# The head of a load queue: image 0's first 32 rows in three transfers of 8, 8 and 16 rows instead of one

## The chip, the cores and the metric

One core of a Trainium2 chip runs the program. The time is device microseconds of one execution; medians of several runs are given. The profile's span is about 1.2 us shorter than that time (82.0 us against 83.26 in the run that was profiled before the change), and all instants below are counted from the span's start.

The engines' names: PE is TensorE, DVE VectorE, ACT ScalarE, POOL GpSimd; SP (SyncE) only issues transfers. A transfer is cut into packets, which the 16 DMA engines of the core move. It has landed when all 16 have added to its semaphore. The records name neither the engine of a packet nor that of a landing; where this text speaks of one engine's lag, it goes by the order of the 16 landings.

## The reference, cut to what matters

```
x: (8, 32, 128, 128) float32
out = x + conv3x3(groupnorm(x, 16 groups), weight, bias)      # padding 1
```

The convolution is written with an FFT of 256 and a crop that begins at 64, so that only a part of the image gets anything from it. The kernel holds each image as 128 partitions (channel, row parity, column parity) of 64 x 64 numbers. Each image's statistics are needed before its convolution, and all 16.8 MB are read and written once.

## The kernel before

SP issues all loads at the start, in order: image 0 in two halves of 32 rows (1 MB each, 8,192 bytes per partition), images 1 to 3 (2 MB each), two pairs (4 MB each). Each load has a semaphore of its own. ACT issues the weights. (Here and below `[...]` marks a cut.)

```python
    def load(to, of, by="sp"):
        name = f"load{len(put.sems)}"
        put.semaphore(name)
        return put(by, lambda e: e.dma_start(to, of), adds=name)

    loaded[0] = []
    for half in range(2):
        rows = slice(half * H // 2, (half + 1) * H // 2)
        loaded[0].append((rows.stop, load(xts[0][:, rows, :], x[0, :, 0, rows, :])))
        if half == 0:
            weights_in = load(wb_sb, wb, by="act")
    for img in range(1, 4):
        loaded[img] = [(H, load(xts[img], x[img // 2, :, img % 2]))]
    for pair in range(2, NPAIR):
        loaded[2 * pair] = loaded[2 * pair + 1] = [(H, load(pairs[pair], x[pair]))]
```

The first consumers are sums (DVE) and sums of squares (ACT) of image 0's first half, then of its second half, then the normalization and the convolution on TensorE. Before the convolution TensorE does a small matmul on image 1's first element, so it waits for image 1 as well. Results are written in place and stored by SP:

```python
    def pilot(img):
        pilot_ok[img] = put(
            "pe", lambda e: e.matmul(ps_w[:, img : img + 1], avg, xts[img][:, 0, 0:1], start=True, stop=True),
            *rows_in(img, 1), avg_ok, mark=True,
        )
    # [...]
    group(0, 1)
    warm_ok = keep_warm(0, 1, w_ok)
    pilot(1)
    take_std(0)
    normalize(0)
    # [...] per image: multiply, add, store
            if img == 2 or img == 4:
                store(out[img // 2 - 1], pairs[img // 2 - 1], *finished(img - 2, img - 1))
```

## Time and profile before

| | before |
|---|---|
| time, median of 3 runs | 83.2 us (83.17 to 83.45) |
| span | 82.0 us |
| bytes moved | 33.62 MB, 410 GB/s over the span |
| DMA engines busy | 97.2% of the span on average |
| first packet; last landing | 1.84 us; 81.96 us |

The prediction shows the lines and how to read them. The point to hold on to: the 16 DMA engines are busy without a pause from 2.5 to 80.5 us, so the time is the length of the transfer stream.

### The profile page before, as it was taken

How to read it: one execution, taken by the hardware profiler on the slowest of the kernel's cores; microseconds unless marked ns; L12 is line 12 of the kernel's file. 1: busy time of each engine (PE TensorE's matmuls, PEld its weight loads, DVE VectorE, ACT ScalarE, POOL GpSimd, SP SyncE). 2: the span in 40 equal slices, each digit the busy share in tenths (PEclk: the TensorE clock that was granted, in tenths of full speed). 3: DMA queues.
4: the chain of work that ended last, by engine and by line, in shares of the span. 5: the costliest groups of instructions: out<-in, count | busy, mean ns of one | idle time of the engine just before them, and what ended most of it. 6: DMA issues, size and time to landing. Idle time of an engine off the chain costs nothing.

```text
span 82.0 us, 686 instructions
## 1 busy us (share of the span) xinstructions
PE 66.8 (81%) x222; PEld 41.3 (50%) x222; DVE 50.2 (61%) x43; ACT 47.9 (58%) x53; POOL 31.6 (39%) x43
## 2 busy tenths in 40 slices
PE   0009974999999999999999999999999999993000
PEld 0005433566666666666666656666666666660000
DVE  0009936960899499769949995996899324006000
ACT  3307967981699299569947974994798260000000
POOL 6876000004069900106992930490085029400000
PEclk9999998579999999999999999999999999999965
DMA  2899999999979979979959889989979999999995
GB/s 40 299 415 443 463 415 423 447 407 423 551 304 511 479 320 479 511 336 431 511 256 511 383 383 511 447 352 479 463 336 423 423 431 439 431 423 419 397 430 239
DMA packets 2164, 33.62 MB, mean 410 GB/s; under 512 B 296, under 2 KB 330, under 8 KB 500
## 3 DMA queue, kind: packets, MB, share of 16 engines
q1 hardware_dynamic: 2020, 33.36, 96.3%
q0 software_dynamic: 96, 0.19, 0.6%
q10 hardware_dynamic: 48, 0.06, 0.3%
HBM read 16.84 MB, written 16.78 MB: 410 GB/s over the span
## 4 chain that ended last, share of the span: by engine, by line
PE 74%; DMA 14%; DVE 2%; SPq 1%; issue 0%
PE ps L412 73%; DMA x<-x_dram 14%; DVE x L428 2%; PE ps_m L318 1%; SPq L183 1%; PE ps_w L265 0%
## 5 line engine op out<-in xcount | busy, mean ns | idle before, releaser
L412 PE MATMUL ps<-g,w_sb 128*128 128x363 f32 (+1 forms) x192 | 60.7, 473 | 0.1
L412 PEld LDWEIGHTS ps<-g,w_sb 128*128 128x128 f32 x192 | 36.1, 194 | 20.0 <-ACT origin L292 1.4
L283 DVE TENSOR_REDUCE sums<-x 128x1 f32<-128x4096 f32 x7 | 30.9, 4411 | 0.6 <-DMA x<-x_dram 0.6
L394 POOL TENSOR_SCALAR x<-x,bias_sb 128x1984 f32<-128x1984 f32 (+3 forms) x12 | 23.2, 1945 | 18.9 <-ACT origin L292 14.6
L303 ACT ACTIVATE unused<-x,origin 128x4096 f32<-128x4096 f32 (+1 forms) x9 | 30.0, 3330 | 0.3
L428 DVE SCALAR_TENSOR_TENSOR x<-ps,bias_sb,x 128x1089 f32<-128x1089 f32 (+2 forms) x9 | 10.9, 1220 | 7.7 <-PE ps L412 7.7
L373 ACT ACTIVATE g<-x,rstd 128x1089 f32<-128x1089 f32 (+2 forms) x8 | 9.4, 1190 | 3.4 <-DVE rstd L347 3.4
L283 DVE TENSOR_REDUCE first_sums<-x 128x1 f32<-128x2048 f32 x2 | 4.6, 2286 | 6.2 <-DMA x<-x_dram 6.2
L258 POOL COPY sums<-x 128x1 f32<-128x1 f32 x6 | 1.0, 186 | 18.2 <-DMA x<-x_dram 18.2
L335 DVE TENSOR_SCALAR var<-ps_m,square 128x1 f32<-128x1 f32 x8 | 1.8, 219 | 8.2 <-ACT square L330 8.2
L265 PE MATMUL ps_w<-x,avg 128*128 128x1 f32 x4 | 0.9, 304 | 7.1 <-POOL w_sb L476 6.1
L330 ACT ACTIVATE square<-ps_m,origin 128x1 f32<-128x1 f32 x8 | 2.1, 261 | 7.3 <-PE ps_m L318 7.3
L447 PE MATMUL ps<-x,avg 128*128 128x512 f32 x6 | 4.9, 942 | 0.0
L265 PEld LDWEIGHTS ps_w<-x,avg 128*128 128x128 f32 x4 | 0.8, 248 | 7.9 <-POOL w_sb L476 6.1
L318 PEld LDWEIGHTS ps_m<-sums,avg 128*128 128x128 f32 x16 | 2.8, 188 | 2.2 <-DVE x L428 1.0
L341 ACT ACTIVATE std<-var,eps 128x1 f32<-128x1 f32 x8 | 2.4, 294 | 2.3 <-DVE var L335 2.3
L344 DVE RECIPROCAL rstd<-std 128x1 f32<-128x1 f32 x8 | 1.3, 164 | 2.9 <-ACT std L341 2.9
L292 ACT ACTIVATE origin<-ps_w 128x1 f32<-128x1 f32 x2 | 0.3, 160 | 4.0 <-PE ps_w L265 4.0
L476 POOL COPY w_sb<-wb_sb 32x128 f32<-32x128 f32 (+1 forms) x8 | 2.5, 340 | 0.0
L318 PE MATMUL ps_m<-sums,avg 128*128 128x3 f32 x16 | 2.3, 214 | 0.0
L447 PEld LDWEIGHTS ps<-x,avg 128*128 128x128 f32 x6 | 1.5, 287 | 1.0 <-issue 1.0
L237 ACT ACT_TABLE_LOAD x1 | 1.3, 1283 | 1.2 <-PEq L579 1.2
(21 smaller groups left out, 13.3 us busy)
## 6 DMA issues: line engine op xcount, KB each, us to landing
x<-x_dram SPq DMA_DIRECT2D x2, 4096.0 KB, 34.3
out_dram<-x SPq DMA_DIRECT2D x2, 4096.0 KB
x<-x_dram SPq DMA_DIRECT2D x3, 2048.0 KB, 16.0
out_dram<-x SPq DMA_DIRECT2D x3, 2048.0 KB
x<-x_dram SPq DMA_DIRECT2D x2, 1024.0 KB, 6.2
out_dram<-x SPq DMA_DIRECT2D x1, 1056.0 KB
out_dram<-x SPq DMA_DIRECT2D x1, 800.0 KB
out_dram<-x POOLq DMA_DIRECT2D x1, 189.0 KB, 7.7
```

The lines of the kernel that those rows point to most:

```text
L283: lambda e: e.tensor_reduce(to_sum(img, k)[:, 0:1], piece, mybir.AxisListType.X, ALU.add),
L303: lambda e: e.activation(unused[:, rows.start * W : rows.stop * W], piece, AF.Square, bias=origins[img], accum_out=to_sum(img, k)[:, 1:2],),
L318: lambda e: e.matmul(ps_ms[:, 0 : of.shape[1]], avg, of, start=(part == 0), stop=(part == last)),
L330: lambda e: e.activation(squares[img], ps_ms[:, 0:1], AF.Square, bias=origins[img]),
L335: lambda e: e.tensor_scalar(variances[img], ps_ms[:, 1:2], squares[img], None, op0=ALU.subtract),
L341: lambda e: e.activation(stds[img], variances[img], AF.Sqrt, bias=eps, scale=float(FFT * FFT)),
L373: lambda e: e.activation(g[:, rows, :], xt[:, LO + rows.start : LO + rows.stop, LO:W], AF.Identity, bias=rstd[:, 1:2], scale=rstd[:, 0:1],),
L394: put("pool", lambda e: e.tensor_scalar(part, part, 1.0, bias_sb, op0=ALU.mult, op1=ALU.add), *free, mark=mark)
L412: lambda e, k=k, dc=dc, rows=rows, top=top: e.matmul(ps[:, 0:rows, 0 : N - dc], w_sb[:, k * P : (k + 1) * P], g[:, top : top + rows, dc:N] ...
L428: lambda e: e.scalar_tensor_tensor(part, in0=ps, scalar=bias_sb, in1=part, op0=ALU.add, op1=ALU.add),
L447: "pe", lambda e: e.matmul(pss[1][:, 0, :], avg, piece, start=True, stop=True),
L476: lambda e: e.tensor_copy(w5[to, :, dc, :, c.start * C : c.stop * C], taps[:, 1 - rin : 5 - rin, b, :].rearrange("p (dr r) b o -> p dr r ( ...
```

## The change

The intent, as it can be read from it: begin with small transfers, so that the stream gets going sooner, and grow them. The consumers still wait for all three (the semaphore counts to 48). The weights' load is written first, which changes nothing in its queue.

```diff
+PIECES = (8, 8, 16), (32,)
 [...]
-    def load(to, of, by="sp"):
+    def load(*transfers, by="sp"):
         name = f"load{len(put.sems)}"
         put.semaphore(name)
-        return put(by, lambda e: e.dma_start(to, of), adds=name)
-
-    loaded[0] = []
-    for half in range(2):
-        rows = slice(half * H // 2, (half + 1) * H // 2)
-        loaded[0].append((rows.stop, load(xts[0][:, rows, :], x[0, :, 0, rows, :])))
-        if half == 0:
-            weights_in = load(wb_sb, wb, by="act")
+
+        return [put(by, lambda e: e.dma_start(to, of), adds=name) for to, of in transfers][-1]
+
+    weights_in = load((wb_sb, wb), by="act")
+
+    loaded[0], first = [], 0
+    for pieces in PIECES:
+        transfers = []
+        for piece in pieces:
+            rows = slice(first, first + piece)
+            transfers.append((xts[0][:, rows, :], x[0, :, 0, rows, :]))
+            first = rows.stop
+        loaded[0].append((first, load(*transfers)))
 [...]  # the other loads pass their pair of patterns as one argument
```

More of the change, by code (lines that the diff above doesn't have):

```diff
@@ L178, in conv_preact_kernel @@
     loaded = {}
-    def load(to, of, by="sp"):
+    def load(*transfers, by="sp"):
         name = f"load{len(put.sems)}"
         put.semaphore(name)
-        return put(by, lambda e: e.dma_start(to, of), adds=name)
-    loaded[0] = []
-    for half in range(2):
-        rows = slice(half * H // 2, (half + 1) * H // 2)
-        loaded[0].append((rows.stop, load(xts[0][:, rows, :], x[0, :, 0, rows, :])))
-        if half == 0:
-            weights_in = load(wb_sb, wb, by="act")
+        return [put(by, lambda e: e.dma_start(to, of), adds=name) for to, of in transfers][-1]
[8 more added lines that the diff above has]
+        loaded[0].append((first, load(*transfers)))
     for img in range(1, 4):
-        loaded[img] = [(H, load(xts[img], x[img // 2, :, img % 2]))]
+        loaded[img] = [(H, load((xts[img], x[img // 2, :, img % 2])))]
     for pair in range(2, NPAIR):
-        loaded[2 * pair] = loaded[2 * pair + 1] = [(H, load(pairs[pair], x[pair]))]
+        loaded[2 * pair] = loaded[2 * pair + 1] = [(H, load((pairs[pair], x[pair])))]
     def rows_in(img, last):
```

## The prediction

> **What bounds the kernel now.** I read the page's clock and DMA rows first, then the DMA queues, then stretches of time, and only then the chain of waits, because a kernel that moves 33.6 MB in 82 us is a suspect for being limited by the DMA engines however busy TensorE looks.
>
> The page, parts 1 to 3: TensorE's busy share, then (in slices of 2.05 us) the granted clock, the DMA engines' busy share and the rate, then the queues with their share of all 16 engines' time.
>
> ```profile
> PE 66.8 (81%) x222; PEld 41.3 (50%) x222; DVE 50.2 (61%) x43; ACT 47.9 (58%) x53; POOL 31.6 (39%) x43
> ...
> PEclk9999998579999999999999999999999999999965
> DMA  2899999999979979979959889989979999999995
> ...
> q1 hardware_dynamic: 2020, 33.36, 96.3%
> q0 software_dynamic: 96, 0.19, 0.6%
> q10 hardware_dynamic: 48, 0.06, 0.3%
> HBM read 16.84 MB, written 16.78 MB: 410 GB/s over the span
> ```
>
> The shares of the queues add up to 97.2% of the span: on average each DMA engine is busy for 79.7 of 82.0 us. Stretches of time (columns: stretch, length, busy us of PE, weight loads, DVE, ACT, POOL, granted clock, DMA share, GB/s) show where the other 2.3 us lie:
>
> ```profile
> 0.00:1.80 1.80, 0.00 (x0) 0.00 (x0) 0.00 (x0) 0.55 (x1) 1.11 (x7) 1.00 0.00 0
> 1.80:3.00 1.20, 0.00 (x0) 0.00 (x0) 0.00 (x0) 0.93 (x2) 1.05 (x3) 1.00 0.90 179
> 3.00:13.40 10.40, 5.76 (x13) 2.81 (x13) 5.21 (x6) 5.43 (x8) 3.93 (x15) 1.00 1.03 435
> 13.40:42.00 28.60, 28.53 (x97) 18.13 (x97) 22.95 (x16) 21.96 (x23) 11.26 (x9) 0.94 1.00 423
> 42.00:79.50 37.50, 32.55 (x116) 20.35 (x115) 22.06 (x22) 19.01 (x21) 14.23 (x12) 0.99 1.00 430
> 79.50:82.00 2.50, 0.00 (x0) 0.00 (x0) 0.00 (x0) 0.00 (x0) 0.00 (x0) 0.50 0.63 267
> ```
>
> The reader is to see three things: nothing moves before 1.8 us; from 1.8 to 3.0 the engines count as busy at 179 GB/s only (a slow start); from 3.0 to 79.5 their share is 1.00 or more (a packet is booked where it begins) at 423 to 435 GB/s. The single packet records say the same: the first begins at 1.84, in every whole microsecond from 2.5 to 80.5 the 16 engines are busy, the last ends at 81.62. So the transfer stream never runs dry, and the kernel is as long as that stream.
>
> The chain of waits tells another story, and I do not follow it:
>
> ```profile
> 1.73 11.62 DMA x<-x_dram
> 13.34 0.04 issue
> 13.39 0.38 PE ps_w L265 x2
> 13.77 0.07 issue
> 13.84 6.14 PE ps L412 x14
> ...
> 71.55 3.01 PE ps L412 x10
> 74.56 0.02 issue
> 74.58 1.48 DVE x L428 x2
> ```
>
> It passes from image 1's landing through TensorE without a gap to the last add at 76.06; the last store is issued after that, and all lands at 81.96. But the last store is 1,056 KB, which at 430 GB/s takes 2.5 us, not 5.9. It stands behind earlier stores: its first data packet begins at 77.98 in the packet records. A transfer's first packet came 1.02 us after its issue began (0.81 to 1.84), so a store issued at 76.09 could have begun at about 77.1. TensorE's chain thus has some 0.9 us to spare at the end, the tightest place; the other stores are issued 2.7 us or more before the transfers in front of them have landed.
>
> **What the Trainium skill says.** (1) "DMA: Bandwidth & Descriptors", section "Why a DMA increments its semaphore by 16 and not by 1": with two transfers in flight on one semaphore a count that would suit the first alone may be filled by the second; only the sum of all is safe. The change waits for the sum, 48, so it is correct, and nothing can start after the first 8 rows. The trace agrees on the counting: one load gives 16 landings (5.53 to 5.97 us for the first). (2) Same page, "Why small descriptors are slow (HBM only)": each packet has a fixed cost. The trace agrees and sizes it: packets of 32,768, 16,384, 8,192 and 1,984 bytes took 1,213, 611, 309 and 81 ns in steady flow, a line of 0.0367 ns per byte plus 8 to 9 ns. (3) Same page, "Latency and other measured facts": about 0.6 us to the first byte. Here the first packet came 0.64 us after the issuing instruction ended (1.20 to 1.84). (4) "TensorE: Matmul & The Clock Gate", Part 1: windows of 3.4 us that run freely. In this trace the first convolution's matmuls run at half clock from 13.83 to 17.24, a whole window; other executions may lose less, but by the paragraph above that time is hidden.
>
> **The change part by part.** The weights' load is written first in the program, but it was and is issued on ACT's queue at 0.81, beside SP's first: nothing moves. SP's order stays image 0, image 0, image 1 and so on. One 1 MB transfer of the first half (128 rows of 8,192 bytes, 8 packets on each engine) becomes transfers with 2,048, 2,048 and 4,096 bytes per partition, 8 packets each on each engine.
>
> Packet time per engine before: 8 x 309 = 2,472 ns. After, by the line of point 2 (estimates from those four sizes): 16 x 83.5 = 1,336 and 8 x 159 = 1,272, together 2,608 ns. Cost +0.14 us. Two more completion records of 4 bytes (9 ns in the records, some 17 with the gaps around them): +0.03 us. All of it lies on the bounding stream: +0.17 us.
>
> SP's issuing: seven loads took 3.53 us, 0.50 us each with pauses; the first two are 0.44 us apart. Two more delay the second half's issue from 1.25 to about 2.15 and the later ones by 0.9 us. Is the stream starved? Pieces would be ready 1.02 us after their issues at 0.81, 1.25 and 1.7: at 1.84, 2.28 and 2.7. At full rate the first piece keeps an engine busy until 1.84 + 0.67 = 2.51, the second until 3.18, the third until 4.45; the second half is ready at about 3.2, image 1 at 3.7. Each is ready before the one in front is finished, by at least 0.2 us, more if the start is slow. Cost of the extra issues: 0.
>
> The slow start is the one place of gain. Of the first packets 19 of 8,192 bytes took far over 309 ns (up to 1,167). Their excess, summed over those begun before 3.1 us, is 8.4 us over 16 engines, 0.52 us per engine, and 0.06 for the weights'. Were it due to the wait for a first whole packet of 8,192 bytes before the engine's write side has work, packets of 2,048 would shorten the fill by 309 - 83 = 0.23 us. Were it a plain latency or a joint limit of all engines, nothing would be saved. Nothing in this trace decides; I take half to all of the 0.23, since a small first piece is the only sense I can see in this change: about -0.2 us. Removing all of the excess would give -0.58, the most there is.
>
> Sum: +0.17 - 0.2 = about 0; taken with a slight lean to the intent, 83.2 - 0.1 = 83.1 us.
>
> The compute side: the first half's sums begin when all three pieces have landed, at 5.99 + 0.17 less the gain. Its chain (squares, variance, normalization, 12.78) moves by a tenth or so, and the convolution follows image 1's landing (13.34), which moves with the stream. With 0.9 us to spare at the end none of that sets the time.
>
> **The rivals.** (a) The small pieces are slow at HBM. Partitions lie 32 KB apart in the source, so the first piece reads only the first 2 KB of every 32 KB; if the 179 GB/s of the start come from engines that walk the same addresses in step, 0.5 MB in such pieces could stay at that rate: 2.9 us instead of 1.3, so +1.6 us, about 84.8. For it: the first 16 packets all drag and then all run at 309 ns. Against it: the 8,192-byte rows at the same pitch run at full rate from 3.0 on. I give it 4%. (b) Starvation at the start because small transfers are drained faster than SP issues (0.45 us against 0.67 us of data). Against it the sums above; if an issue took 0.63 us, as one did (the fourth), a gap of 0.1 to 0.2 us: 83.4. (c) TensorE bound after all, as the chain of waits has it: then image 1's landing decides, later by 0.17 less the gain; a delayed start falls into the half-clock window and costs half of itself, and an earlier one pays in full. 82.9 to 83.3, the same verdict. (d) The slow start is nearly all removed: 82.7.
>
> **Range and chances.** The runs before spread from 83.17 to 83.45. Gains are bounded by the excess of 0.58 us, so faster by 2% (1.66 us) has no mechanism: 2%. A slowdown of 1.66 us needs rival (a) in full: 3%. Everything else is within 2%. Eight times in ten between 82.6 and 83.6.
>
> **What would show it right or wrong.** In the changed kernel's trace: the DMA share at 1.00 from 3 us to the end with no dip before 6 us (against rival b); GB/s in the stretch from 1.8 to 3.0 at or above 179 (against a); packets of 2,048 bytes at 83 ns and 4,096 at 159 (the +0.14); first sums at 5.8 to 6.2 and image 1's landing at 13.2 to 13.5 instead of 13.34, and the span changed by the same amount. The prediction is wrong if the time moves by much more than image 1's landing does, if the pieces stay slow after 3 us, or if the end moves with TensorE's last matmul while the stream has gaps.

## The result, and the profile after

| | before | changed |
|---|---|---|
| time, median of 6 runs | 83.22 us (83.14 to 83.45) | 84.41 us (84.15 to 84.73) |
| ratio of the fast runs, 95% interval | | 1.0135 (1.0107 to 1.0163) |
| span of the profiled run | 82.0 us | 82.9 us |
| image 1 landed, mean of the 16 engines / last engine | 13.11 / 13.34 us | 13.93 / 14.70 us |
| last store landed, mean / last engine | 81.60 / 81.96 us | 82.03 / 82.86 us |

A ratio is the mean time of one kernel's fast runs over that of the other's fast runs of the same rounds, so it is not quite the ratio of the medians. The change cost 1.2 us, and the prediction's range ended at 83.6. It is a loss clear of the noise, and still under 2%. The changed kernel's profile is of its fastest run, 84.15 us, so the traces below account for 0.9 us of the 1.2.

The changed kernel's page, the rows that answer to those of before:

```profile
PEclk9999999999999999999999999999999999999755
DMA  0999999999999999899989999999979999999993
...
q1 hardware_dynamic: 2308, 33.36, 95.5%
```

The same stretches of the changed kernel (columns as in the prediction; the last two are the DMA engines' share and GB/s):

```profile
1.80:3.00 1.20, 0.00 (x0) 0.00 (x0) 0.00 (x0) 0.94 (x2) 1.05 (x3) 1.00 0.75 213
3.00:13.40 10.40, 5.54 (x11) 3.21 (x12) 4.79 (x3) 4.62 (x7) 3.86 (x15) 1.00 1.02 390
13.40:42.00 28.60, 28.58 (x96) 17.42 (x95) 23.36 (x18) 22.88 (x24) 10.95 (x9) 1.00 1.02 437
42.00:79.50 37.50, 32.84 (x118) 20.55 (x116) 22.05 (x23) 19.02 (x21) 14.58 (x12) 0.98 0.99 426
79.50:82.90 3.40, 0.00 (x0) 0.00 (x0) 0.00 (x0) 0.00 (x0) 0.00 (x0) 0.50 0.59 250
```

The reader is to see that the kernel is still one transfer stream with almost no gap (shares of about 1.00 from 3 us on; counted from the packets, an engine had none for 0.12 us on average from 3 to 80 us, most of it at 4.8 to 5.9), and that the loss lies in one line: from 3.0 to 13.4 us it runs at 390 GB/s where it ran at 435. The first 1.2 us are better than before, 213 against 179. Cut into single microseconds, before and then changed:

```profile
4.00:5.00 1.00, 0.00 (x0) 0.00 (x0) 0.00 (x0) 0.00 (x0) 0.55 (x4) 1.00 1.03 434
5.00:6.00 1.00, 0.00 (x0) 0.00 (x0) 0.01 (x1) 0.00 (x0) 0.94 (x4) 1.00 1.00 418
6.00:7.00 1.00, 0.90 (x3) 0.93 (x4) 1.00 (x1) 0.27 (x2) 0.88 (x5) 1.00 1.02 426
```

```profile
4.00:5.00 1.00, 0.00 (x0) 0.00 (x0) 0.00 (x0) 0.00 (x0) 0.94 (x6) 1.00 1.10 377
5.00:6.00 1.00, 0.00 (x0) 0.00 (x0) 0.00 (x0) 0.00 (x0) 0.94 (x5) 1.00 1.18 234
6.00:7.00 1.00, 0.07 (x1) 0.10 (x1) 0.18 (x1) 0.00 (x0) 0.94 (x4) 1.00 0.72 283
```

A second slow spell stands at 5 to 7 us, with the engines "busy" at half the rate. In the packet records it is made mostly of the first 8,192-byte packets of image 0's second half: they begin at 4.93 us and take up to 1,733 ns instead of 309, while others take the normal time. The small packets ahead of them ran as predicted (84 ns for 2,048 bytes, 159 for 4,096), but for a few of 4,096 bytes from 4.5 us on (up to 775 ns).

A useful measure is the excess: what a packet took beyond 0.0367 ns per byte plus 8.5 ns, summed over all engines' packets and divided by 16.

| packets begun in | before | changed |
|---|---|---|
| 1 to 3 us (the slow start) | 0.57 us | 0.24 us |
| 3 to 12 us | 0.09 | 1.00 |
| 12 to 40 us | 0.19 | 0.09 |
| 40 to 48 us (from loads to stores) | 0.46 | 0.05 |
| 48 us to the end | 0.11 | 0.11 |

So the intended gain is there, 0.33 us at the start, and is more than given back: 0.9 us in the second spell. Some 0.4 us of it is regained at the switch from loads to stores (in this pair of profiles; why is not shown), and over the whole span the excess grew by less than 0.1 us. Yet the end is 0.9 us later. In this pair of profiles the 0.9 us are, about: +0.21 us of packet time per engine (79.69 to 79.90, most of it the small packets' own cost), +0.24 us in which an engine had no packet (0.12 before 3 us, 0.12 after), and +0.47 us of lag of the last landing behind the mean. Image 1's last landing was 0.23 us behind the mean before and 0.77 behind it after, and the last store 0.36 and 0.83. Each engine has its own share of every transfer, and the stream ends with the slowest. In the changed kernel every load from image 0's second half (9.80) to the first pair (34.22) has its last landing 0.76 or 0.77 us behind its mean: a lag got at 5 us is carried along.

The changed chain of waits, its beginning:

```profile
2.19 7.61 DMA x<-x_dram
9.80 0.02 issue
9.82 2.30 DVE first_sums L289
...
14.74 0.59 PE ps_w L271 x2
15.33 4.94 PE ps L418 x14
```

The convolution began at 15.2 us instead of 13.84, behind the second half's sums. Even so the last store's issue moved only from 76.09 to 76.39 us, because this run's convolution left the half clock sooner: two matmuls, at 15.20 and 15.94 us, took 944 and 730 ns, those from 16.50 on about 460, so it ran at half clock for 1.3 us, before the change for 3.4. (The page's PEclk row doesn't show that: its clock record begins at 16.46 us, and the time before counts as full.) The last store's first data packet was at 78.47: TensorE still had about 1 us to spare (a first packet follows its issue by 1.02 us).

### The profile page after: what moved, and what is told of

Same layout as the page of the kernel before. It is cut to its first block, busy times and chain, and to the rows that moved or that the text cites. A ratio compares the mean times of both kernels' runs of the same rounds, so it can differ in the third digit from the quotient of the medians.

```text
span 82.9 us, 688 instructions
## 1 busy us (share of the span) xinstructions
PE 67.0 (81%) x222; PEld 41.2 (50%) x222; DVE 50.2 (61%) x43; ACT 48.0 (58%) x53; POOL 31.6 (38%) x43
## 4 chain that ended last, share of the span: by engine, by line
PE 75%; DMA 9%; DVE 5%; SPq 1%; issue 0%
PE ps L418 71%; DMA x<-x_dram 9%; DVE first_sums L289 3%; PE ps L453 2%; PE ps_m L324 2%; DVE x L434 2%; SPq L185 1%; PE ps_w L271 1%
## 5 line engine op out<-in xcount | busy, mean ns | idle before, releaser
L418 PE MATMUL ps<-g,w_sb 128*128 128x363 f32 (+1 forms) x192 | 59.6, 466 | 0.0
L418 PEld LDWEIGHTS ps<-g,w_sb 128*128 128x128 f32 x192 | 35.5, 191 | 19.4 <-ACT origin L298 1.4
L453 PE MATMUL ps<-x,avg 128*128 128x512 f32 x6 | 5.8, 1108 | 0.0
L324 PEld LDWEIGHTS ps_m<-first_sums,avg 128*128 128x128 f32 x4 | 1.2, 324 | 2.0 <-ACT unused L309 1.5
```

The source lines that it names most:

```text
L324: lambda e: e.matmul(ps_ms[:, 0 : of.shape[1]], avg, of, start=(part == 0), stop=(part == last)),
L418: lambda e, k=k, dc=dc, rows=rows, top=top: e.matmul(ps[:, 0:rows, 0 : N - dc], w_sb[:, k * P : (k + 1) * P], g[:, top : top + rows, dc:N] ...
L453: "pe", lambda e: e.matmul(pss[1][:, 0, :], avg, piece, start=True, stop=True),
```

## The experiments

In all of them the base is the changed kernel; "one transfer" means its variant with (32,), (32,). Theories, as the expectations name them. A: engines stall when they step from small packets to 8,192-byte ones. B: the cost is in the number of transfers, by SP's issues. C: each transfer's descriptors reach the engines only about 1.1 us after those of the one before, so small transfers at the head leave the engines without. D: engines walk the same memory addresses in step. F: they stall while SP issues further transfers behind small ones. H: short transfers in the first microseconds, with little queued behind them, upset the engines.

**Undo the pieces, keep the rest.**

```diff
-PIECES = (8, 8, 16), (32,)
+PIECES = (32,), (32,)
```

> The changed kernel with its first 32 rows in one transfer again, all else of the change kept (the weights' load written first, its semaphore numbered before the others). Every theory that blames the small pieces, by their packets or by their number: 83.2 us as before, a slow start from 1.8 to 3.0 us and none at 5 us. If the renumbering or the order were the cause: 84.4 us, as changed.

83.35 us against 83.29 before in the same rounds, ratio 1.0001 (0.9975 to 1.0028), and no spell at 5 us (410 GB/s from 5 to 6). The pieces are the cause, not the order or the semaphores' numbers.

**Three transfers with large packets.**

```diff
-        for piece in pieces:
-            rows = slice(first, first + piece)
-            transfers.append((xts[0][:, rows, :], x[0, :, 0, rows, :]))
 [...]
+        parts_of = (slice(0, 32), slice(32, 64), slice(64, P)) if first == 0 else (slice(0, P),)
+        transfers = [(xts[0][of, rows, :], x[0, of, 0, rows, :]) for of in parts_of]
```

> Three transfers on one semaphore as in the change, but cut by partitions (32, 32 and 64), so that all packets keep 8,192 bytes. Theory A (packets: the engines stall when they step from small packets to 8,192 bytes): no second slow spell at 5 us, 83.2 to 83.4 us. Theory B (number of transfers and issues of SP): the spell at 4.5 to 6.8 us as in the changed kernel, 84.2 to 84.6 us.

85.0 us, 1.0207 (1.0174 to 1.024). This looks like B, but it isn't a clean test: the packets took long from the first to the last of the three transfers (187, 262, 213, 254 and 180 GB/s in the microseconds from 2 to 7), not only after them. A transfer that reaches 32 or 64 of the partitions ran at half rate here, which is a cost of its own. The run says that cutting by partitions is bad, and nothing on A or B. So short transfers with large packets at full rate stay untested.

**Small packets in two long transfers**, each with two blocks of 2,048 bytes per partition (rows 0 to 7 and 16 to 23, then the others):

```diff
+            to = xts[0][:, rows, :].rearrange("p (a b r) w -> p b a (r w)", a=2, b=2)
+            of = x[0, :, 0, rows, :].rearrange("p (a b r) w -> p b a (r w)", a=2, b=2)
+            transfers = [(to[:, k], of[:, k]) for k in range(2)]
 [...]  # the second half stays one transfer
```

> Two transfers for the first 32 rows, each with two blocks of 2,048 bytes per partition, rows 0-7 and 16-23, then 8-15 and 24-31: 32 packets of 2,048 bytes on each engine from two issues, then the second half in packets of 8,192. Theory A: a slow spell where the 8,192-byte packets begin, 84.2 to 84.8 us. Theory B (issues): about half of the change's loss, 83.8 us. If only the cost per packet counts: 83.2 + 0.2 = 83.4 us.

83.63 us, 1.0042 (1.0016 to 1.0068). All the first 32 rows came in packets of 2,048 bytes, more than in the change, and the loss is a third of it, close to the 0.2 us that the packets themselves cost. The slow start was longer (excess 0.71 us) and what came after 3 us, the step to 8,192 bytes in it, cost 0.24 (0.09 before the change). Small packets alone are not it.

**Both halves in small pieces**: `PIECES = (8, 8, 16), (8, 8, 16)`.

> Both halves of image 0 in pieces of 8, 8 and 16 rows. Theory A: the second half's 2,048-byte packets start without a stall, and the slow spell moves to where image 1's packets of 16,384 bytes begin, about 8 to 10 us, perhaps a smaller one at each step up; 84.4 to 85 us. A theory of time or place (something at 5 us, or the second half's addresses): the spell stays at 4.5 to 6.8 us.

84.13 us, 1.009 (1.0058 to 1.0122). The excess of 3 to 12 us is 0.93 us, spread over several beginnings of transfers (packets of 4,096 bytes with up to 1,072 ns at 3.9 and 1,005 at 6.8), so it is no spell that hangs on one address or one moment. The profile is of the slowest run (84.72), in which the convolution ran at half clock from 15.26 to 21.42 us and the stores waited for it too: the engines had 0.25 us without work at 52 us, and another slow start behind it (excess 0.57 us from 48 us on). So not all of that run's time is the pieces'.

**The same small pieces, but behind the first megabyte**: `PIECES = (32,), (8, 8, 16)`.

> The pieces moved behind the data: first 32 rows in one transfer, the second half in 8, 8 and 16. As many transfers, packets and bytes as in the change. Theory A (a stall where small packets are followed by large ones): the slow spell comes where image 1 begins, at about 8 us, 84.2 to 84.6 us. Theory C (each transfer's descriptors reach the engines only about 1.1 us after those of the transfer before, so small transfers at the head run the engines dry, but not behind 2.5 us of data): only the packets' own cost of 0.17 us remains, 83.3 to 83.6 us, no spell after 3 us.

83.23 us, 0.9998 (0.9967 to 1.0029): nothing lost, not even clearly the 0.17 us. Its stretches where the small pieces run and image 1 follows:

```profile
5.00:6.00 1.00, 0.00 (x0) 0.01 (x1) 0.09 (x1) 0.00 (x0) 0.89 (x5) 1.00 0.94 363
6.00:7.00 1.00, 0.98 (x3) 0.92 (x4) 1.00 (x1) 0.35 (x2) 0.94 (x5) 1.00 1.09 416
```

No stretch is near 234 GB/s. The number, the sizes and the completion records of the transfers are those of the change, only their place differs. A and B fall here; what remains is what C had said, within 0.1 us.

**Two of 16 rows**: `PIECES = (16, 16), (32,)`.

> First 32 rows in two transfers of 16. Theory C: one transfer fewer ahead of the second half than in the change, its descriptors come some 1.1 us sooner, against a stall of about 0.6 us in the change: 83.3 to 83.6 us. Theory A: 4,096-byte packets are followed by 8,192 as in the change, 84.2 to 84.5 us.

83.34 us, 1.0016 (0.9983 to 1.0049). No second spell (excess of 3 to 12 us: 0.14). As C said.

**Four of 8 rows**: `PIECES = (8, 8, 8, 8), (32,)`.

> First 32 rows in four transfers of 8. Theory C: one transfer more ahead of the second half, and about the same bytes: 1 us more than the change, 85.2 to 85.7 us, image 1 landing about 1 us later than in the change. Theory A: a similar stall as in the change, 84.3 to 84.8 us.

85.17 us, 1.0211 (1.0172 to 1.025). The time is what C said, its mechanism is not: image 1's mean landing was 13.52 us, earlier than in the change, and C wanted it 1 us later. Thirteen of 16 engines landed it at 13.08 to 13.41, as before the change; the other three at 13.94, 14.76 and 15.29. The loss is the lag of a few engines, and it was there before the second half: the last two landings of the first 32 rows came at 6.94 and 7.90, all others by 6.05. Here most of the excess after 3 us, 0.36 of 0.54 us, fell on 2,048-byte packets (up to 811 ns), not on the 8,192-byte ones.

**The second piece on ACT's queue.**

```diff
+        queues = [by, "act", by] if len(transfers) == 3 else [by] * len(transfers)
+        return [put(q, lambda e: e.dma_start(to, of), adds=name) for q, (to, of) in zip(queues, transfers)][-1]
```

> The change, but the second transfer of 8 rows is issued on ACT's queue, behind the weights. Theory C with a limit for each queue: only three transfers of SP up to the second half, 83.4 to 83.8 us. Theory C with one limit for all queues: 84.2 to 84.6 us as in the change. Theory A: as in the change.

83.70 us, 1.0052 (1.0006 to 1.0097): more than half of the loss is gone, with the same three transfers. Image 1 landed at 13.10 (mean) and 13.51 (last). C with a limit for each queue had said so.

**The descriptors' rate by itself**: eight transfers of one row, 256 bytes per partition, ahead of image 0 (one transfer for each half).

```diff
+    tiny = sbuf("tiny", P, 8, W)
+    tiny_in = load(*((tiny[:, k, :], x[0, :, 0, k, :]) for k in range(8)))
 [...]  # PIECES of one transfer each; the first store also waits for tiny_in
```

> Measures the disputed rate by itself: eight transfers of one row (256 bytes per partition, 8 packets of 256 bytes on each engine) go ahead of image 0 on SP's queue, then all as in the one-transfer control. Their data would take some 0.15 us each, so the engines wait for descriptors and the beginnings of their packets show when each transfer's descriptors arrive. Theory C: about 1.1 us between one transfer and the next, image 0's first packet after 10 us. If descriptors keep pace with SP's issues: 0.45 us between them, image 0's first packet at about 5.4 us; then theory C falls as it was put. Time: 83.3 plus that shift.

One look (state unknown), 87.24 us. SP's issues, then two stretches:

```profile
0.81 3.71 SPq L185 DMA_DIRECT2D tiny<-x_dram  x8
4.57 3.67 SPq L185 DMA_DIRECT2D x<-x_dram  x7
```

```profile
6.00:7.00 1.00, 0.00 (x0) 0.00 (x0) 0.00 (x0) 0.00 (x0) 0.94 (x4) 1.00 0.83 262
7.00:8.00 1.00, 0.00 (x0) 0.00 (x0) 0.00 (x0) 0.00 (x0) 0.11 (x1) 1.00 1.03 410
```

Eight issues in 3.76 us (0.81 to 4.57) are 0.47 us each. Image 0's first packet came at 5.63, which is 1.06 us after its issue began at 4.57, as at the very start. Descriptors keep pace with the issues, and C falls as it was put, although the times of four runs above were in its range or within 0.1 us of it. The second pair of lines shows something else: the large packets that begin at 5.63 have a slow start (excess 0.57 us, single packets up to 1,233 ns) although the engines had been moving tiny packets since 1.83. In this kernel the slow start belongs to the first large packets, not to the first microseconds.

**Later issues held back** until the first 32 rows have landed:

```diff
 [...]  # load passes `needs` on to put
-        loaded[img] = [(H, load((xts[img], x[img // 2, :, img % 2])))]
+        loaded[img] = [(H, load((xts[img], x[img // 2, :, img % 2]), needs=[loaded[0][0][1]]))]
```

> The change, but SP issues image 1 and all later loads only once the first 32 rows have landed (at about 5.5 to 6 us, in time for their data at about 8). Theory C (the second half's descriptors come late): it is still the fourth transfer, so the spell at 4.5 to 6.8 us stays and the time is 84.2 to 84.7 us. Theory F (engines stall while SP is still issuing further transfers behind a run of small ones): no issues at that time, no spell, 83.3 to 83.7 us.

86.11 us, 1.0301 (1.0233 to 1.0369); a time that neither theory had given; the profiled run was slow, so only its first microseconds are used. No issue of SP lay between 2.93 and 6.7 us, and the spell was there: excess 0.69 us in packets begun from 5 to 6. F falls. Image 1, now nearly late itself, paid another slow start (0.34 us from 7 to 10).

**The changed kernel once more.**

> The changed kernel a second time, for another profile: 84.2 to 84.7 us. If the slow packets have a fixed cause in the order of transfers, they are again the first ones of the second half, at 4.5 to 6.8 us, on many engines; if engines stall at random while small transfers run, they lie elsewhere and the slowest engine's lag differs.

84.84 us in one look (state unknown). Its stretch:

```profile
5.00:6.00 1.00, 0.00 (x0) 0.00 (x0) 0.00 (x0) 0.00 (x0) 0.94 (x5) 1.00 1.23 274
```

The spell is at the same place (excess 0.24 us at the start, 0.92 later, against 0.24 and 1.00), the slowest engine lagged by 1.19 us at image 1 and by 1.27 at the last store. In both profiles the place is the same and the size of the lag is not; that would fit this kernel's wider spread of times, but two profiles don't show it.

**Four of 16 rows**: `PIECES = (16, 16), (16, 16)`.

> All of image 0 in four transfers of 16 rows, 1.27 us of data each. As many transfers before image 1 as the kernel with two halves of three pieces has before its fifth. Theory C: data of a transfer last longer than the 1.1 us to the next one's descriptors, no spell: 83.3 to 83.6 us. A theory in which the number of transfers or of semaphore records is the cost: 84.2 us or more.

83.44 us, 1.0023 (0.9997 to 1.0048), no spell. Five transfers up to image 1 and eight packets each of 4,096 bytes cost next to nothing if each transfer carries 1.27 us of data.

**Another pitch of the source**, 4,352 bytes of padding behind each partition's 32 KB, for one transfer, for the change and for four of 8:

```diff
+    arrays["x_dram"] = np.pad(arrays["x_dram"], ((0, 0), (0, 0), (0, PAD)))      # PAD = 1088
+    x = x[:, :, 0 : 2 * H * W].rearrange("n p (b h w) -> n p b h w", b=2, h=H)
 [...]  # the shapes that follow from it
```

> The one-transfer control with 4,352 bytes of unused padding behind each partition's 32 KB in the source, so that the rows that the engines read at one time no longer lie at the same place of every 32 KB. Theory D (engines in step on the same addresses obstruct each other; the slow start pulls them apart): the slow start shrinks from 0.6-0.7 us per engine to 0.2 or less, time 82.7 to 83.0 us. If the place in memory has no part: 83.2 to 83.4 us and the slow start as before.

> The change with the same padding. Theory D: no spell at 4.9 to 6.8 us, 82.8 to 83.4 us. If the place in memory has no part: the spell stays, 84.2 to 84.7 us.

> Four pieces of 8 rows with the same padding, against 85.2 us without. Theory D: no engine lags, 83.0 to 83.6 us. If the place in memory has no part: 84.8 to 85.7 us.

83.40, 84.16 and 84.98 us, ratios 1.0029 (0.9966 to 1.0092), 1.0095 (1.0052 to 1.0138) and 1.0159 (1.0083 to 1.0235). The slow start stayed (0.58 us against 0.60 without padding), and so did the spell of the padded change:

```profile
5.00:6.00 1.00, 0.00 (x0) 0.00 (x0) 0.00 (x0) 0.00 (x0) 0.94 (x5) 1.00 1.06 217
```

D falls.

**8 and 24 rows**: `PIECES = (8, 24), (32,)`.

> First 32 rows in two transfers of 8 and 24, no padding. Theory D: the first 2,048-byte packets pass quickly, then the 6,144-byte packets are the first large ones and have the spell, at 2.8 to 4 us: 83.4 to 84.2 us. If a run of several small transfers is needed: as the control, 83.2 to 83.5 us.

83.80 us, 1.0048 (0.9996 to 1.0101). In the range that D gave, though D had already fallen by its own test: the 6,144-byte packets had a small spell at once (0.14 us from 3 to 4), and the excess of 1 to 12 us is 0.55 us, no more than with one transfer (0.73). One short transfer seems only to move the slow start; image 1 landed at 13.51 on its last engine. The interval includes no loss at all.

**Order 16, 8, 8**: `PIECES = (16, 8, 8), (32,)`.

> The change's three pieces in the order 16, 8, 8: same packets, same bytes, and the second half is still the fourth transfer of SP. Theory H (small transfers in the first microseconds, while little is queued behind them, upset the engines): 1.27 us of data at the head, no spell, 83.2 to 83.7 us. If the cause is that the second half follows three transfers of 2.6 us in all (its descriptors late): the spell at 5 us stays, 84.2 to 84.7 us.

83.85 us, 1.0058 (1.0017 to 1.0098): neither of the two. More than half of the loss is gone with the same packets and the same place of the second half in the queue. The profile is of its slowest run (84.55) and has a weaker spell, 0.50 us from 3 to 12; in it too the convolution was long at half clock (15.15 to 20.39 us) and stores waited (an excess of 0.51 us from 48 us on, against 0.11).

**Tiny transfers behind the first megabyte**, to see whether descriptors keep pace while data flow:

```diff
         loaded[0].append((first, load(*transfers)))
+        if len(loaded[0]) == 1:
+            tiny_in = load(*((tiny[:, k, :], x[0, :, 0, k, :]) for k in range(8)))
 [...]  # as above
```

> Eight transfers of one row (256 bytes per partition) behind the first 1 MB transfer and ahead of the second half. If descriptors keep pace with SP's issues (0.47 us) under load, those of the tiny ones wait when the 1 MB is through at about 5 us: their packets run back to back within about 1 us, and the second half, issued at about 5.0, starts at 6.1. If under load each transfer takes about 1.1 us, the tiny ones come 1 us apart until about 10 us, and the time is 87 us or more. In the first case about 84.5 us.

One look (state unknown), 87.21 us. The packets of the tiny transfers ran back to back, nearly all between 5.0 and 6.5 us, so descriptors keep pace under load too. The time I had put to that case was wrong. The second half, issued at 5.13, arrived at 6.2 to engines with nothing left to do, and paid a slow start (excess 0.69 us from 3 to 12), with one engine landing it at 11.32 us when the other 15 had it by 10.24.

**What they say together.** The first 32 rows, by what stands at the head of SP's queue:

| first 32 rows | 8-row transfers on SP | time | ratio |
|---|---|---|---|
| 32 | 0 | 83.35 us | 1.0001 |
| 16, 16 | 0 | 83.34 | 1.0016 |
| 8, 24 | 1 | 83.80 | 1.0048 |
| 8 on SP, 8 on ACT, 16 | 1 | 83.70 | 1.0052 |
| 16, 8, 8 | 2 | 83.85 | 1.0058 |
| 8, 8, 16 (the change) | 2 | 84.41 | 1.0135 |
| 8, 8, 8, 8 | 4 | 85.17 | 1.0211 |
| 32, and the second half in 8, 8, 16 | none at the head | 83.23 | 0.9998 |

The loss grows with the number of short transfers (0.67 us of data each by the packet records, against 0.47 us for an issue of SP) that follow one another at the head of one queue; it is absent when they stand behind 2.5 us of data, and absent when each carries 1.27 us. That is H in its outline: the ends of this table are shown, while the intervals of the rows from 16, 16 to 16, 8, 8 overlap, so that their order is not. What happens inside the engines is not shown: why packets are slow at the beginning at all, and why they are slow again after short transfers, unevenly, mostly the first large ones but with four of 8 the small ones. The runs exclude packet size alone, the number of transfers or completion records alone, the rate of descriptors, later issues and the row pitch. Short transfers always came with 2,048-byte packets here (the cut by partitions was no clean test), so that the shortness alone does it is not shown. The kernels with a full slow start (excess 0.5 to 0.6 us from 1 to 3 us) mostly ran clean afterwards, and most that slipped through with 0.2 to 0.4 paid later; but 16, 8, 8 paid both, and the one with a piece on ACT's queue little of either (0.30 and 0.17), so this is a pattern and no law.

No version beats the kernel before.

## Why the prediction was wrong

**What bounds the kernel.** Right. The engines had next to no gap between 3 and 80 us in the changed kernel (0.12 us on average), and in the profiled run TensorE's late start (15.2 us) didn't set the end. But the argument was made for the mean engine. "On average each DMA engine is busy for 79.7 of 82.0 us" was true, the mean busy time rose only to 79.9, and the end moved by 0.9 us: 0.47 of it because the slowest engine's lag rose (0.36 to 0.83 us at the last landing). A lag of single engines was not in the sum. That the change would stay within 2%, given 95 in 100, was right.

**The packets' cost**, +0.14 us, was right: 84 and 159 ns measured, 83.5 and 159 used. The 9-ns completion records are there as well.

**No starvation.** "Cost of the extra issues: 0" was too low. Issue and delivery keep 0.47 us per transfer with idle engines, and the tiny transfers behind the first megabyte show no sign of their being slower under load. But the margin of "at least 0.2 us" did not keep every engine in work: the engines had 0.12 us more without a packet before 3 us (share 0.75 against 0.90), and 0.12 us between 3 and 6 us, although the second half had been issued at 2.19. Issue times don't explain that second gap; its cause stays open.

**The slow start is the one place of gain.** This is the step that failed. The gain itself was found, and larger than predicted: excess down by 0.33 us, where I had put -0.2. (The mechanism offered for it, the wait for a first whole packet, was tested by no run.) What I assumed in silence is that a slow start, once past, is past. The sentence "Were it a plain latency or a joint limit of all engines, nothing would be saved" weighed only gain or no gain; it had no case in which it comes again. It came again, mostly with the first 8,192-byte packets of the second half, 0.9 us per engine and unevenly, and left the slowest engine 0.77 us behind the mean at image 1. The term of the sum that should have stood there is missing. Why it comes again stays open.

**The rivals.** (a) had small pieces slow at memory and in step; nearly all of the pieces' packets ran at full speed, and padding refuted the addresses. (b) happened in part: the gaps are about the 0.1 to 0.2 us that it gave, but not for the reason that it gave. (c) did not happen in the profiled run. (d) was the opposite of what happened. The range of 82.6 to 83.6 was built from these alone, so a loss of 1.2 us had no place but in (a).

**The checks I named** mostly worked: GB/s from 1.8 to 3.0 at 213, packets of 84 and 159 ns, and two that failed and so showed where the loss begins: the first sums at 6.8 us instead of 5.8 to 6.2, and image 1's landing later than 13.5. The three signs of being wrong did not appear: pieces slow after 3 us, the end moving with TensorE, the time moving much more than image 1's landing. They asked for other mechanisms than the one that came. "And the span changed by the same amount" was off: image 1's last landing moved by 1.36 us and the span by 0.9, with about 0.4 us regained at the switch from loads to stores.

## What to carry to other kernels

Where a kernel is one long transfer stream, look at the slowest DMA engine, not at the mean: here a lag got in the first microseconds lasted to the last store. (Where the stores had to wait for the convolution it shrank: from 0.73 us at image 1 to 0.39 at the end with both halves in small pieces.) Put large transfers first and small ones behind them; here pieces of 256 KB behind a megabyte were free, and the same pieces at the head cost 1.2 us, while pieces of 512 KB at the head were free too. And don't cut a transfer whose pieces nobody uses one by one: sharing a semaphore, the three pieces could start no consumer sooner.

## What the Trainium skill lacked or had wrong

- "DMA: Bandwidth & Descriptors", rules for kernel authors, asks for 1 MiB or more per transfer for bandwidth. It doesn't say that the place in the queue decides: pieces of 256 KB cost 1.2 us at the head (84.41 us) and nothing behind 1 MB of data (83.23 us).
- No page has the slow start of a stream's first large packets (8,192 bytes in up to 1,167 ns against 309, some 0.57 us per engine), or that it returns later after short transfers (up to 1,733 ns at 5.6 us).
- "DMA: Bandwidth & Descriptors", on completion: it says that engines finish on their own, but not that their spread is kept along a queue. Image 1's last engine was 0.77 us behind the mean at 14.7 us, the last store's 0.83 us at 82.9.
- The same page's row on HBM pitch at large powers of two is about copies between HBM tensors at far larger pitches (512 KiB and up). At 32 KB no effect of the pitch was seen: padded, 83.40 and 84.16 us (ratios 1.0029 and 1.0095), against 83.35 and 84.41 (1.0001 and 1.0135, intervals overlapping).
- No page gives the time of an issue on SP ("DMA: Bandwidth & Descriptors" has one in sequencer cycles, for earlier chips as a whole): 0.47 us per transfer of 128 partitions, eight in a row; single ones took up to 1.3 us.
- "TensorE: Matmul & The Clock Gate", Part 1, has the free-running window of 3.4 us right: the clock records here last 3.413 us or whole multiples of it, but for the last one, which the end cuts. A start varied by more than one window, though: counted from its first matmul, the convolution ran at half clock for 1.3 us (the changed kernel) to 6.2 us (both halves in small pieces), for 3.4 in the kernel before. Where it lasted over 5 us and the convolution began after 15 us (three profiles), the engines were without a packet for 0.08 to 0.37 us between 48 and 60 us.
